# Layer 2 attention scores of a four-layer model: weighted spectra made four products ahead, one sample pair's softmax between the other pair's products

## The chip, the cores and the metric

The kernel runs on one core of a Trainium2 chip, in one launch. The metric is the device time of that launch in microseconds (us). A core has TensorE (PE, matrix products, with its weight loads listed as PEld), VectorE (DVE), ScalarE (ACT), GpSimd (POOL), and SyncE (SP), which here only issues transfers. All data are 32-bit floats. Engines run their own instruction lists in order and wait for each other through semaphores.

## The reference

The input is x of shape (4, 56, 56, 128). Four layers follow one another, each as `x = x + layer(groupnorm(x))`: window and full attention with an MLP, an edge layer, a spectral attention (layer 2), and a small convolution. The change is in layer 2. It sees each of the 4 samples as 56 images t of 56 x 128 and does, with 32 heads:

```python
k = _fno_layer(xa_n, wK, ...)     # spectral convolution to half size, 32 heads
q = _fno_layer(xa_n, wQ, ...)
v = _fno_layer(xa_n, wV, ...)     # full size
scores = einsum('bhtd,bhsd->bhts', qs, ks) / sqrt(d)
attn_w = softmax(scores, axis=-1)
out = einsum('bhts,bhsd->bhtd', attn_w, vs)
projd = _fno_layer(out, wP, ...)  # back to one image
attention = _inorm(projd + xa, ...)
```

followed by two more spectral layers. An `_fno_layer` multiplies an image's low frequencies with weights of the head, transforms back, and adds a weighted copy of the image (the skip).

## The kernel before

The kernel never makes q and k. By Parseval's theorem a score is a sum over frequencies: the image spectra of t times those of s, weighted per head and frequency with a product of the two weight sets. `spectra` (a function before the change) leaves in on-chip memory, for two sample pairs `bp` and two samples `b2` in the two halves of 64 partitions, `st.S` (spectra in 16 columns c, 56 times t), `st.iS` (the same times i), `st.R` (17 columns of the other frequencies, which only the skips need), and in device memory `st.apart` (four rows that need an own product). `all_score_weights` leaves the weights `st.g`, `st.g4`.

`attention_weights` (L1383 and on) then works for each sample pair:

- skips (L1411 to L1421): 17 columns, for each sample two matmuls of 64 x 64 tiles into `q_pg`; ScalarE copies (L1420) and GpSimd multiplies with `ww`, per head (L1421), into `q_sc`.
- weighted spectra `q_u` (128 partitions x 32 heads x 56): for each column c a real one (n=0) and an imaginary one (n=1). The real ones are made by VectorE (L1448), which reads the spectrum from a copy `q_px` in the matmul banks (PSUM); GpSimd makes the imaginary ones from `st.iS` for c below 12 (L1445), VectorE the last four. Each tag of `q_u` has three buffers.
- products (`add`, L1435): each `q_u` is multiplied with `st.S` by 8 matmuls, over two row halves (the two samples) and two column halves of PE's array, into `q_acc`, four banks. After the 32 of S come four with `T` and `Tp`, from VectorE (L1454), over all 128 rows.
- softmax (L1458 to L1467): VectorE adds `q_acc` to `q_sc`, reduces, subtracts, ScalarE takes the exponential, VectorE reduces, inverts and multiplies.

After both pairs, all scores are transposed into `st.AT` (L1477, copies by VectorE and ScalarE in turn), `eye` is made by GpSimd, and 32 matmuls with it give `AbT`, the mixing matrix (L1490). Order in this stage comes from a scheduler that places instructions by priority, save where `manual_schedule` holds engines to program order.

`attend` follows: 24 turns of weighting the value spectra `xh` with `u_d`, rows of a table `dd` that SP loads and spreads over partitions (L1517), by VectorE (L1544, from a copy `u_px` that ScalarE makes, L1528) and GpSimd (L1546), and of matmuls with `st.AT` (L1549). PE and ScalarE are held to program order here. In the middle of each turn it runs a step of `mix_images`, which mixes the input images with `AbT` and writes them out: 18 steps.

On-chip memory is a stack from the left and one from the right. A tile that takes freed memory waits for the last use of what lay there. `q_T`, `q_Tp`, `q_sc` and the `q_u` lie left, over the memory of the spectra stage; `u_d` takes it after them.

Of the kernel before, what the change touches and what calls it, by code (L numbers as in the profile page):

```python
# [18 lines left out]
P = 128  # L19
# [1364 lines left out]
def attention_weights(k, I, w, st):  # L1384
# [4 lines left out]

    nc, tc = k.nc, k.tc  # L1390
    g, g4 = st.g, st.g4
    with ExitStack() as es:
        big = es.enter_context(tc.tile_pool(name="q_big", bufs=1))
        wks = ExitStack()
        wk = wks.enter_context(tc.tile_pool(name="q_wk", bufs=2))
# [8 lines left out]
        nc.vector.tensor_mul(ww, w.qksh[:, 0, :], w.qksh[:, 1, :])  # L1404
        pv = big.tile([112, 16], F32, name="q_pv")
        nc.vector.tensor_mul(pv, w.pva[:, 0, :], w.pva[:, 1, :])
        halves = (slice(0, 64), slice(64, 128))
        sc = big.tile([P, B, 16, HH], F32, name="q_sc")

        with tc.tile_pool(name="q_ps0", bufs=2, space=PSUM) as psum:  # L1410
            for bp in range(2):  # L1411
                pg = [psum.tile([P, 512], F32, name="q_pg%d" % b2) for b2 in range(2)]
                for c in range(17):
                    for b2 in range(2):
                        r = st.R[halves[b2], bp, c, :]
                        for o in halves:
                            nc.tensor.matmul(pg[b2][o, :HH], r, r[:, :HH], start=(c == 0), stop=(c == 16))
                for b2 in range(2):
                    g0 = wk.tile([P, HH], F32, name="q_g0")
                    nc.scalar.copy(g0, pg[b2][:, :HH])  # L1420
                    nc.gpsimd.tensor_mul(sc[:, 2 * bp + b2], bc(g0, 1, 16), bc(ww, 2, HH))  # L1421
        with tc.tile_pool(name="q_ps", bufs=1, space=PSUM) as psum:
            for bp in range(2):
                px = psum.tile([P, 3, 512], F32, name="q_px")
                for i in range(2):
                    nc.scalar.copy(px[:, i, :NB].rearrange("p (c t) -> p c t", t=HH), st.S[:, bp, 8 * i:8 * i + 8, :HH])
                nc.scalar.copy(px[:, 2, :4 * HH].rearrange("p (c t) -> p c t", t=HH), st.iS[:, bp, 12:16, :HH])
                acc = psum.tile([P, 4, 512], F32, name="q_acc")

                def add(u, x, rows, b2, start=False, stop=False):  # L1430
                    for hb in range(4):
                        for i in range(2):
                            if b2 is None or b2 == i:
                                o = halves[i] if rows is None else rows
                                nc.tensor.matmul(acc[halves[hb % 2], 2 * i + hb // 2, :NB], x[o],  # L1435
                                                 u[o, 8 * hb:8 * hb + 8, :].rearrange("p h t -> p (h t)"),
                                                 start=start, stop=stop)


                for c in range(16):  # L1440
                    for n in range(2):
                        u = wk.tile([P, HEADS, HH], F32, tag="u%d" % (n and c < 12), name="q_u", bufs=3)
                        weights = bc(g[:, n, c, :], 2, HH)
                        if n and c < 12:
                            nc.gpsimd.tensor_mul(u, bc(st.iS[:, bp, c, :HH], 1, HEADS), weights)  # L1445
                        else:
                            x = px[:, 2, (c - 12) * HH:] if n else px[:, c // 8, c % 8 * HH:]
                            nc.vector.tensor_mul(u, bc(x[:, :HH], 1, HEADS), weights)  # L1448
                        add(u, st.S[:, bp, c, :], None, None, start=(c == 0 and n == 0))
                for b2 in range(2):  # L1450
                    b = 2 * bp + b2
                    for n in range(2):
                        u = wk.tile([P, HEADS, HH], F32, tag="u0", name="q_u4", bufs=3)
                        nc.vector.tensor_mul(u, bc(Tp[:, n, b, :HH], 1, HEADS), bc(g4[:, n, 0, :], 2, HH))  # L1454
                        add(u, T[:, b, :], slice(0, P), b2, stop=(n == 1))
                scp = sc[:, 2 * bp:2 * bp + 2]
                scf = scp.rearrange("p b (x h) s -> p (b x) (h s)", x=2)
                nc.vector.tensor_add(scf, scf, acc[:, :, :NB])  # L1458
                scf = scp.rearrange("p b i s -> p (b i) s")
                red = wk.tile([P, 2 * 16], F32, tag="red", name="q_red")  # L1460
                nc.vector.tensor_reduce(red, scf, AX.X, ALU.max)
                nc.vector.tensor_sub(scf, scf, bc(red, 2, HH))
                nc.scalar.activation(scf, scf, AF.Exp, scale=1.0 / math.sqrt(ND))
                den = wk.tile([P, 2 * 16], F32, tag="red", name="q_den")
                nc.vector.tensor_reduce(den, scf, AX.X, ALU.add)
                nc.vector.reciprocal(den, den)
                nc.vector.tensor_mul(scf, scf, bc(den, 2, HH))  # L1467
        wks.close()
        big = es.enter_context(tc.tile_pool(name="q_end", bufs=1))
        with tc.tile_pool(name="q_ps1", bufs=2, space=PSUM) as psum:  # L1470
            at = st.AT.rearrange("p (i f) b t -> p b i f t", f=2)
            for b in range(B):
                for i0 in range(0, 8, 4):
                    pt = psum.tile([P, 4, P], F32, name="q_pt")
                    for i in range(4):
                        ii = 2 * (i0 + i)
                        nc.tensor.transpose(pt[:112, i, :], sc[:, b, ii:ii + 2, :].rearrange("p h s -> p (h s)"), k.ident)  # L1477
                    for i in range(4):
                        copy(k, i, at[:, b, i0 + i], pt[:112, i, :].rearrange("p (f t) -> p f t", f=2)[:, :, :at.shape[4]])
            eye = big.tile([112, 16, HH], F32, name="q_eye")  # L1480
            fold = big.tile([112, HH], F32, name="q_fold")
            nc.sync.dma_start(fold[:HH], I["w2_eye"])
            nc.sync.dma_start(fold[HH:], I["w2_eye"])
            nc.gpsimd.tensor_mul(eye, bc(fold, 1, 16), bc(pv, 2, HH))
            pa = psum.tile([P, 2, 64], F32, name="q_pa")
            nc.vector.memset(st.AbT, 0.0)
            for b2 in range(2):
                o = slice(64 * b2, 64 * b2 + HH)
                for hp in range(16):
                    nc.tensor.matmul(pa[o], eye[:, hp, :], st.AT[:, hp, b2::2, :], start=(hp == 0), stop=(hp == 15))  # L1490
                nc.scalar.copy(st.AbT[o], pa[o, :, :HH])


def attend(k, st, dd, xad, xm):

    nc, tc = k.nc, k.tc
# [928 lines left out]
```

## Time and profile before

| | |
|---|---|
| median of 3 runs | 3965.18 us (3956.41 to 3967.73) |
| profiled execution | 3959.12 us, span 3957.3 us |
| granted PE clock, mean | 0.952 |
| busy: PE, DVE, ACT, POOL | 3558.4, 2896.4, 2048.5, 1181.2 us |
| end of the spectra's matmuls, first product `q_acc` | 3037.9, 3054.89 us |
| last division of the softmax begins | 3189.81 us |
| first `u_po` matmul of the value stage | 3219.93 us |

Times inside the span count from its start. A page of the profile gives busy time by engine, the span in 40 slices, the chain of work that ended last, and groups of instructions; the trace can be asked for stretches, single tiles, waits and the timeline. A timeline row reads: start in us, length in us, engine, line, operation, out<-in, shapes, count, and in brackets the idle time before it and what ended that. A tile row gives durations as smallest/median/largest in ns, and first and last start. Matmul lengths are modelled at their end; their starts are measured. Each matmul has two records.

### The profile page before, as it was taken

How to read it: one execution, taken by the hardware profiler on the slowest of the kernel's cores; microseconds unless marked ns; L12 is line 12 of the kernel's file. 1: busy time of each engine (PE TensorE's matmuls, PEld its weight loads, DVE VectorE, ACT ScalarE, POOL GpSimd, SP SyncE). 2: the span in 40 equal slices, each digit the busy share in tenths (PEclk: the TensorE clock that was granted, in tenths of full speed). 3: DMA queues.
4: the chain of work that ended last, by engine and by line, in shares of the span. 5: the costliest groups of instructions: out<-in, count | busy, mean ns of one | idle time of the engine just before them, and what ended most of it. 6: DMA issues, size and time to landing. Idle time of an engine off the chain costs nothing. (4 is left out here: it accounts for less than half of the span.)

```text
span 3957.3 us, 79405 instructions
## 1 busy us (share of the span) xinstructions
PE 3558.4 (90%) x35416; PEld 1586.4 (40%) x35416; DVE 2896.4 (73%) x2678; ACT 2048.5 (52%) x2067; POOL 1181.2 (30%) x664
## 2 busy tenths in 40 slices
PE   6899988989998898999889899998967969999988
PEld 4322234542223445222245532224545333336554
DVE  6588868758887685898778578886874857775664
ACT  4577754557775455777545477764522012215332
POOL 0000007500000670000057000003742648984665
PEclk8999989999999999999999999999977989999988
DMA  2000000000000000000000000000031047832101
GB/s 94 1 1 1 1 1 19 19 1 1 1 1 1 18 19 1 1 1 1 1 18 3 17 1 1 1 1 1 3 132 39 1 94 166 173 90 82 58 9 49
DMA packets 73496, 111.12 MB, mean 28 GB/s; under 512 B 62140, under 2 KB 63932, under 8 KB 67900
## 3 DMA queue, kind: packets, MB, share of 16 engines
q1 hardware_dynamic: 14460, 93.13, 7.9%
q10 hardware_dynamic: 58688, 12.85, 1.9%
q8 instruction: 279, 4.57, 0.5%
q14 instruction: 69, 0.57, 0.0%
HBM read 79.46 MB, written 26.51 MB: 27 GB/s over the span
## 5 line engine op out<-in xcount | busy, mean ns | idle before, releaser
L641 ACT ACTIVATE f_ring<-f_s 128x1792 f32<-128x1792 f32 (+3 forms) x796 | 1097.9, 1429 | 316.9 <-PE f_s L639 314.8
L594 DVE TENSOR_TENSOR f_acc<-f_acc,f_ring 128x1792 f32<-128x1792 f32 x560 | 1134.0, 2025 | 81.1 <-ACT f_ring L641 27.7
L639 PE MATMUL f_s<-f_qT,f_kT 32*128 32x448 f32 x5376 | 740.6, 573 | 57.7 <-ACT f_ring L641 26.6
L883 POOL TENSOR_TENSOR x<-xf,xw 128x343 f32<-128x343 f32 (+2 forms) x36 | 29.9, 832 | 2131.7 <-issue 2059.4
L600 PE MATMUL f_po<-f_ring,f_va 128*32 128x448 f32 x5376 | 592.1, 548 | 0.0
L967 DVE TENSOR_TENSOR e_td<-e_pa,e_c 128x1792 f32<-128x1792 f32 x252 | 491.2, 2012 | 8.0 <-ACT e_a L934 8.0
L969 POOL TENSOR_TENSOR e_tp<-e_a,e_c 128x1792 f32<-128x1792 f32 x140 | 451.7, 3258 | 143.4 <-PE e_acc L974 104.6
L639 PEld LDWEIGHTS f_s<-f_qT,f_kT 32*128 32x128 f32 x5376 | 268.6, 184 | 538.7 <-ACT f_ring L641 369.6
L974 PE MATMUL e_acc<-e_td,t_shared 32*32 32x448 f32 x8064 | 322.3, 545 | 25.3 <-DVE e_td L967 14.8
L971 ACT ACTIVATE e_tp<-e_tp 128x1792 f32<-128x1792 f32 x140 | 235.1, 1697 | 186.6 <-POOL e_tp L969 186.6
L1544 DVE TENSOR_TENSOR u_ud<-u_px,u_d 112x1792 f32<-112x1792 f32 x144 | 240.2, 1707 | 106.3 <-PE u_po L1549 82.7
L600 PEld LDWEIGHTS f_po<-f_ring,f_va 128*32 128x32 f32 x5376 | 133.0, 109 | 399.8 <-issue 398.9
L1549 PE MATMUL u_po<-u_ud,AT 112*64 112x448 f32 x960 | 202.2, 551 | 34.5 <-DVE u_ud L1544 34.5
L974 PE MATMUL e_acc<-e_tp,t_shared 32*32 32x448 f32 x4480 | 220.6, 544 | 2.4 <-ACT e_tp L971 2.2
L1546 POOL TENSOR_TENSOR u_up<-xh,u_d 112x1792 f32<-112x1792 f32 x64 | 193.4, 3046 | 48.2 <-PE u_po L1549 21.2
L974 PEld LDWEIGHTS e_acc<-e_td,t_shared 32*32 32x32 f32 x8064 | 133.6, 103 | 149.8 <-DVE e_td L967 59.9
L594 DVE TENSOR_TENSOR f_acc<-f_ring 128x1792 f32<-128x1792 f32 x28 | 56.7, 2024 | 106.3 <-ACT f_ring L641 77.4
L1549 PEld LDWEIGHTS u_po<-u_ud,AT 112*64 112x64 f32 x960 | 65.2, 138 | 159.6 <-issue 87.5
L1549 PE MATMUL u_po<-u_up,AT 112*64 112x448 f32 x576 | 126.2, 545 | 0.0
L1435 PE MATMUL q_acc<-q_u,S 64*64 64x448 f32 x1024 | 102.6, 557 | 16.6 <-DVE q_u L1448 12.5
L974 PEld LDWEIGHTS e_acc<-e_tp,t_shared 32*32 32x32 f32 x4480 | 94.4, 103 | 54.7 <-ACT e_tp L971 18.5
L1445 POOL TENSOR_TENSOR q_u<-iS,q_g 128x1792 f32<-128x1792 f32 x24 | 77.6, 3268 | 124.5 <-PE s_px L1282 92.8
(462 smaller groups left out, 4721.7 us busy)
## 6 DMA issues: line engine op xcount, KB each, us to landing
u_d<-dd SPq DMA_DIRECT2D x48, 784.0 KB
xw<-in_x SPq DMA_DIRECT2D x4, 1568.0 KB
x2d<-x SPq DMA_DIRECT2D x4, 1568.0 KB
x_xs<-xad ACTq DMA_DIRECT2D x32, 196.0 KB
xm<-x_ev ACTq DMA_DIRECT2D x64, 98.0 KB
o_a<-xm SPq DMA_DIRECT2D x8, 784.0 KB
o_x<-x2d SPq DMA_DIRECT2D x4, 1568.0 KB
out<-o_o SPq DMA_DIRECT2D x12, 448.0 KB
```

What stands on the lines that cost most here:

```text
L594: nc.vector.tensor_add(acc, slots(j, 0) if c == 1 else acc, slots(j, c))
L600: nc.tensor.matmul(po[heads[h], :NB], va[o, c, heads[h]], p, start=(c == 0), stop=(c == 24))
L639: nc.tensor.matmul(ss[:, i, :NB], kT[heads[h], c * P:(c + 1) * P], qT[heads[h], blk(j)], start=True, stop=True)
L641: nc.scalar.activation(ring[:, slot:slot + m, :], ss[:, :m, :NB], AF.Exp, scale=scale)
L967: nc.vector.tensor_tensor(t, am, cm, ALU.max)
L969: nc.gpsimd.tensor_sub(t, bc(a.rearrange("p (l n) -> p l n", l=8), 1, 4), cm)
L971: nc.scalar.activation(tf, tf, AF.Relu)
L974: nc.tensor.matmul(acc[quarters[q], r, :NB], k.ident[o, o], t[o, q].rearrange("p l n -> p (l n)"), start=(g == 0), stop=(g == len(EDGE_TUR ...
L1435: nc.tensor.matmul(acc[halves[hb % 2], 2 * i + hb // 2, :NB], x[o], u[o, 8 * hb:8 * hb + 8, :].rearrange("p h t -> p (h t)"), start=start, ...
L1544: nc.vector.tensor_mul(u, bc(px[:, :, :NB], 2, m), dm)
L1546: nc.gpsimd.tensor_mul(u, bc(x, 2, m), dm)
L1549: nc.tensor.matmul(po[64 * b2:64 * b2 + 64, :NB], st.AT[:, 8 * i + h0 + q, 2 * bp + b2, :], u[:, b2, q, :], start=(left == 16), stop=(left ...
```

## The change

- One list `seq` holds 36 products for each pair; a `T` product stands before the imaginary one of every fourth column.
- `make` is called for the product four places further on before each product. Copies `q_px` are made for eight columns at a time, in two buffers. All imaginary `q_u` are made by GpSimd.
- `product` loops over the sample outside and the four head blocks inside. Each sample has its own `q_acc` of two banks, one buffer.
- `skips`, `softmax` and the transposes are generators that advance one step after each product from the fourth on: the skips of both pairs between the products of the first pair, the softmax and transposes of the first pair between those of the second. VectorE multiplies the skips with `ww`, straight from `q_pg`; the softmax works on one sample at a time; ScalarE alone copies transposes, four at once.
- Four engines are held to program order in the whole stage.
- `q_T`, `q_Tp`, `q_ww` and `q_sc` lie right.
- `pv`, `fold`, `eye` and the `AbT` matmuls go to `mix_images`, in its first and a new second step (19 steps now); the matmuls alternate between the column halves. The memset of `AbT` is GpSimd's.

```diff
-        big = es.enter_context(tc.tile_pool(name="q_big", bufs=1))
-        wks = ExitStack()
-        wk = wks.enter_context(tc.tile_pool(name="q_wk", bufs=2))
+        big = es.enter_context(tc.tile_pool(name="q_big", bufs=1, side="right"))
+        wk = es.enter_context(tc.tile_pool(name="q_wk", bufs=2))
+        psum = es.enter_context(tc.tile_pool(name="q_ps", bufs=2, space=PSUM))
...
+        es.enter_context(tc.manual_schedule(engines={mybir.EngineType.PE, mybir.EngineType.Activation,
+                                                      mybir.EngineType.DVE, mybir.EngineType.Pool}))
+        px, made, acc = {}, {}, {}
+        seq = []
+        for bp in range(2):
+            for c in range(16):
+                seq += [(bp, c, 0, None), (bp, c, 1, None)]
+                if c % 4 == 3:
+                    seq.insert(len(seq) - 1, (bp, None, c // 4 % 2, c // 8))
+
+        def make(bp, c, n, b2):
+            if b2 is None and n == 0 and c % 8 == 0:
+                px[bp, c // 8] = t = psum.tile([P, 512], F32, tag="x", name="q_px")
+                nc.scalar.copy(t[:, :NB].rearrange("p (c t) -> p c t", t=HH), st.S[:, bp, c:c + 8, :HH])
+            u = wk.tile([P, HEADS, HH], F32, tag="u%d" % (b2 is None and n), name="q_u", bufs=3)
+            if b2 is not None:
+                nc.vector.tensor_mul(u, bc(Tp[:, n, 2 * bp + b2, :HH], 1, HEADS), bc(g4[:, n, 0, :], 2, HH))
+            elif n:
+                nc.gpsimd.tensor_mul(u, bc(st.iS[:, bp, c, :HH], 1, HEADS), bc(g[:, n, c, :], 2, HH))
+            else:
+                nc.vector.tensor_mul(u, bc(px[bp, c // 8][:, c % 8 * HH:c % 8 * HH + HH], 1, HEADS),
+                                     bc(g[:, n, c, :], 2, HH))
...
+        def product(bp, c, n, b2):
...
+                acc[bp] = [psum.tile([P, 2, 512], F32, tag="acc%d" % i, name="q_acc", bufs=1) for i in range(2)]
+            for i in range(2):
+                if b2 is None or b2 == i:
+                    x, o = (st.S[:, bp, c, :], halves[i]) if b2 is None else (T[:, 2 * bp + b2, :], slice(0, P))
+                    for hb in range(4):
+                        nc.tensor.matmul(acc[bp][i][halves[hb % 2], hb // 2, :NB], x[o],
+                                         u[o, 8 * hb:8 * hb + 8, :].rearrange("p h t -> p (h t)"),
+                                         start=first, stop=last)
...
+        def softmax(bp, copies):
+            red, den = {}, {}
+            for i in range(2):
+                red[i] = wk.tile([P, 16], F32, tag="red", name="q_red")
+                nc.vector.tensor_reduce(red[i], sc[:, 2 * bp + i], AX.X, ALU.max)
+                nc.vector.tensor_sub(sc[:, 2 * bp + i], sc[:, 2 * bp + i], bc(red[i], 2, HH))
+                nc.scalar.activation(sc[:, 2 * bp + i], sc[:, 2 * bp + i], AF.Exp, scale=1.0 / math.sqrt(ND))
+                yield
+            for i in range(2):
+                den[i] = wk.tile([P, 16], F32, tag="den", name="q_den")
+                nc.vector.tensor_reduce(den[i], sc[:, 2 * bp + i], AX.X, ALU.add)
+                nc.vector.reciprocal(den[i], den[i])
+                nc.vector.tensor_mul(sc[:, 2 * bp + i], sc[:, 2 * bp + i], bc(den[i], 2, HH))
+                yield
...
+                    for q in range(4):
...
+                    copies(at[:, b, i0:i0 + 4], pt[:112].rearrange("p i (f t) -> p i f t", f=2))
+                    yield
+
+        between = [skips(0), skips(1)]
+        ahead = 4
+        for item in seq[:ahead]:
+            make(*item)
+        for n, item in enumerate(seq):
+            if n + ahead < len(seq):
+                make(*seq[n + ahead])
+            product(*item)
+            if item[1:3] == (15, 1):
+                for i in range(2):
+                    collect(item[0], i)
+                between.append(softmax(item[0], nc.scalar.copy))
+            if n >= 3 and between and next(between[0], 0) == 0:
+                between.pop(0)
...
 def mix_images(k, I, w, st, wk, psum, xad, xm):
...
+    eye = wk.tile([P, 2, 8, HH], F32, tag="x_ev", name="x_eye", bufs=1)[:112].rearrange("p b w h -> p (b w) h")
+    nc.gpsimd.tensor_mul(eye, bc(fold, 1, 16), bc(pv, 2, HH))
     load(0)
     load(1)
+    yield
+    pa = bank()
+    for hp in range(16):
+        for b2, o in enumerate(halves):
+            nc.tensor.matmul(pa[o, 0, :2 * 64].rearrange("p (b t) -> p b t", b=2), eye[:, hp, :], st.AT[:, hp, b2::2, :],
+                             start=(hp == 0), stop=(hp == 15))
+    for o in halves:
+        nc.scalar.copy(st.AbT[o], pa[o, 0, :2 * 64].rearrange("p (b t) -> p b t", b=2)[:, :, :HH])
```

## The prediction

> **What bounds the kernel now.** I first read the table of stretches, to find the stage that the change touches and which engine fills it. Columns: length of the stretch, busy time and records of each engine, granted TensorE clock, DMA share.
>
> ```profile
> core 0: us, PE busy (x) PEld busy (x) DVE busy (x) ACT busy (x) POOL busy (x), PEclk, DMA share, GB/s
> 3038.00:3055.00 17.00, 4.52 (x276) 4.29 (x280) 2.45 (x4) 2.68 (x8) 16.07 (x7) 0.80 0.09 25
> 3055.00:3108.00 53.00, 52.32 (x520) 18.95 (x520) 41.43 (x22) 2.71 (x4) 37.86 (x12) 0.97 0.01 1
> 3108.00:3118.00 10.00, 5.38 (x28) 1.66 (x32) 10.00 (x7) 0.00 (x0) 0.00 (x0) 0.92 0.00 1
> 3118.00:3130.00 12.00, 12.00 (x104) 4.31 (x104) 11.90 (x7) 1.70 (x1) 6.14 (x2) 0.78 0.00 1
> 3130.00:3181.00 51.00, 46.59 (x448) 16.99 (x440) 43.20 (x23) 0.00 (x0) 24.06 (x8) 1.00 0.00 1
> 3181.00:3198.00 17.00, 7.33 (x33) 5.17 (x34) 12.26 (x22) 5.59 (x17) 5.75 (x3) 0.61 0.01 3
> 3198.00:3208.00 10.00, 9.11 (x64) 8.61 (x64) 0.00 (x0) 0.74 (x3) 0.00 (x0) 0.82 0.00 0
> 3208.00:3225.00 17.00, 5.07 (x14) 1.71 (x16) 5.05 (x3) 1.50 (x2) 6.01 (x2) 0.62 0.88 203
> ```
>
> The score stage lies from 3038.6 (last matmul of the spectra) to about 3208. PE is full in the two product stretches. Around them lie 17 us in which GpSimd works (skips) and PE does 4.5 us; 10 us of one sample pair's end; 34 us of softmax, transposes and `AbT`, one after the other; and 12 us of waiting for `u_d`. What ends that last wait is in the chain of waits in order of time (start, length, what):
>
> ```profile
> 3197.85 5.57 PE q_pa L1490 x32
> ...
> 3203.74 3.71 PE q_pa L1490 x32
> ...
> 3207.94 9.52 DMA u_d<-dd
> ...
> 3217.85 2.04 DVE u_ud L1544
> ...
> 3219.93 9.02 PE u_po L1549 x32
> ```
>
> The value stage's first matmul is at 3219.93. It stood behind a load issued at 3207.58 (12.35 us earlier), and the load behind the `AbT` matmuls, whose memory it takes. Then the timeline and the tiles, for durations:
>
> ```profile
> 3064.39 2.02 DVE L1448 TENSOR_TENSOR q_u<-q_px,q_g 128x1792 f32<-128x1792 f32 x1 [0.98 <-PE q_acc L1435]
> ...
> 3094.46 9.75 DVE L1448 TENSOR_TENSOR q_u<-q_px,q_g 128x1792 f32<-128x1792 f32 x5 [0.98 <-PE q_acc L1435]
> ...
> 3117.79 0.30 PEld L1435 LDWEIGHTS q_acc<-q_u,S 64*64 64x64 f32 x8 [4.84 <-DVE q_sc L1458]
> ...
> 3123.86 11.28 POOL L1445 TENSOR_TENSOR q_u<-iS,q_g 128x1792 f32<-128x1792 f32 x3 [26.00 <-PE q_acc L1435]
> ...
> 3127.94 4.15 DVE L1467 TENSOR_TENSOR q_sc<-q_sc,q_den 128x1792 f32<-128x1792 f32 x1
> ```
>
> ```profile
> L1448 DVE TENSOR_TENSOR q_u<-q_px,q_g x40: 2006/2020/2026, 3052.8 to 3167.7; 128x1792 f32<-128x1792 f32 x40
> L1445 POOL TENSOR_TENSOR q_u<-iS,q_g x24: 3187/3195/4975, 3038.2 to 3150.9; 128x1792 f32<-128x1792 f32 x24
> L1467 DVE TENSOR_TENSOR q_sc<-q_sc,q_den x2: 2008/3079/4150, 3127.9 to 3189.8; 128x1792 f32<-128x1792 f32 x2
> ```
>
> From 3064.39 to 3094.46 VectorE is released ten times by PE, each time after two products: 30.07/20 = **1.504 us for a product** at full clock. A weighted spectrum costs 2.02 on VectorE (1.94 start to start in the run of five), 3.16 start to start on GpSimd.
>
> **Part 1: the front.** The first product waits today for skips and all three `px` copies (3054.89). New: one `px` copy (0.54 us, L1426) after ScalarE's last `xh` copy at 3038.55, then 2.02 on VectorE: 3041.2; I take 3041.3. The skips' matmuls come after four products: 136 records a pair, at 223 records in 3.48 us = 2.1 us; I use 2.0 (the row holds a pause). Their products with `ww` go from GpSimd (4 x 1.69) to VectorE, half a big operation (1.0 each), behind PE. `ww`, `pv` and the memset are under 0.2 us, cost nothing, and lie before the products. The loads of `T` and `Tp` (nine on SP, done issuing by 3043.4 today) are first needed at the eighth product, about 3052: hidden.
>
> **Part 2: a sample pair.** 16 re, 16 im and 4 of `T`: 36 x 1.504 = 54.1 us of PE. The four `T` products now stand amid the others and change the tile shape twice each. The nearest row is the first layer's attention: matmuls 0.376 apart, but 0.48 at the change of shape (last L639 start 2301.32, first L600 start 2301.80), so 0.11 a change, 0.9 a pair. Bounds: 0 and 0.2. First pair: 54.1 + 0.9 + 2 skips (4.0) = 59.1, ending **3100.4**. VectorE has there 20 x 1.94 + 4.0 = 43, GpSimd 16 x 3.16 = 51: both hidden by PE, with three buffers each.
>
> All im products on GpSimd (32 instead of 24) and `T` products, subtraction and division on VectorE meanwhile: the division row says what this costs. At 3127.94 it took 4.15 us instead of 2.01, as GpSimd's running operation ended at 3130.2, and GpSimd's next took 4.98. Before, no `T` product or subtraction met GpSimd: it was idle. By the row alone only divisions are charged. The Trainium skill, "SBUF — State Buffer", Who interferes with whom, states that any VectorE instruction with two SBUF inputs locks out a reading GpSimd one, wholly: then the 8 `T` products and 4 subtractions join. By the rule GpSimd needs 32 x 3.16 + 8 x 2.0 + 4 x 1.0 = 121 us, done at 3159, still ahead of PE; by the row 103. I take the rule: a wait before each such VectorE operation of 0 to 3.16, 1.6 taken.
>
> **Part 3: the seam.** One accumulator, so PE waits for both `collect`s (2 x 1.0 + 0.3): 3102.7, against 4.1 today. Softmax of pair 0 then stands between products, in order. VectorE: two collects 2.0, reduce 1.0, subtract 1.0, a product 1.94, reduce, subtract, reduce (3.0), reciprocal 0.25, divide 1.0 = 10.2, plus three waits for GpSimd 4.8 = 15.0, so the first division ends at 3115.6. On PE, four products (6.0) after 3102.7 end at 3108.7; there the first **transpose waits, and all later products behind it, 7.0 us** (2.3 if no wait for GpSimd, 11.7 at the worst waits). Today's stall of 4.07 us before 3117.79 let the clock fall: 0.78 over the next 12 us, 2.6 us lost. I add 2.6 (0 to 3.4). Exps (half of 1.70) run beside VectorE; the table load precedes them.
>
> Second pair: 54.1 + 0.9 + four transpose groups. Each has 8 records of 128 columns, 0.109 apart at full clock (second half of L1490), 0.87, and two shape changes: 1.1. So 59.4. End of products: 3102.7 + 59.4 + 7.0 + 2.6 = **3171.7**.
>
> **Part 4: the tail.** Softmax of pair 1 is bare: eight VectorE half operations (8.2), two reciprocals 0.5, two collects 2.0, hops 0.4: last division ends 3182.8 (from 3179.25 to 3191.82, 12.6 us, today).
>
> The moved step: in the changed program the first `u_d` load waits, on SP, for exactly this division, whose divisor's memory it takes; no longer for transposes and `AbT`. Ahead of it on SP are the two `x_fold` loads (kilobytes), which wait for the last product, earlier. So issue 3182.8, then the same 12.35 to the first `u_po` matmul: **3195.2**. The last transposes and ScalarE's copies (about 5 us), `u_px` behind them on ScalarE (0.9), `eye` and two `u_x` on GpSimd (1.7 + 4.1) lie under the load's 10.3 us; without it, some 6 us would show. The `x_xs` loads on ScalarE's queue come after `u_px`, as before.
>
> Saved: 3219.93 − 3195.2 = 24.7.
>
> **Part 5: given back.** `AbT` moves into the second turn of the value stage, where PE waits only 22 us for VectorE in 335. 64 records alternate two column halves: 64 x 0.109/2 = 3.5 us, plus the wait for two ScalarE copies before `pn` may take the same bank, 0.7: **4.2** (7.7 if the halves don't overlap, 0 if absorbed). Mixing uses 19 of 24 turns instead of 18: nothing.
>
> **Sum.** −24.7 + 4.2 = −20.5. Profiled execution: 3959.12 (span 3957.3) to 3938.6. The median of the runs, 3965.18, lies 6.1 above that execution; I carry the difference over: **3944.7**.
>
> **A rule against the change.** `product` now gives a row half its four matmuls in succession (tiles A B A B C D C D; before A C B D A C B D). The row first: 16 records of a product in four groups of four starts, 0.376 apart, though every matmul has two records. The Trainium skill, "TensorE: Matmul & The Clock Gate", Part 3, says matmuls start and end strictly in program order. Record by record this would make a product 8 groups = 3.0 us in both orders; the row shows 1.504, so the rule doesn't hold for records here. Holding for whole matmuls it lets C start with the second A, D with the second B, and the next A with the second C: again four to a group. I take 1.504.
>
> **Rivals.**
> - *The new order costs PE its overlap* (the other side): if C waits for the second A to finish, a product has 6 groups, 2.26 us; 64 of them cost 48 us more, so 3993. It decides from 20.5/64 = 0.32 us a product, 1.83 us, on. For it: no row shows one tile twice before another row half. Against: the skips, two matmuls per row half in succession, ran four to 62 ns (223 in 3.48 us).
> - *The seam is cheap*: no clock fall, no shape cost, short waits for GpSimd: 2.6 + 2.7 + 4.7 + 1 = 11 less: 3934. For it: ScalarE and PE have little else there. GpSimd's 3159 is the floor.
> - *The seam and waits are dear*: worst waits (+4.7), shape changes at 0.2 (+2), `AbT` not overlapped (+3.5): 3955. For it: GpSimd is almost never idle, so waits are the rule.
>
> **How the numbers follow.** Mine 0.63 (3937 to 3952), cheap seam 0.15, dear 0.15, order 0.07. A measurement tells 0.3% (12 us) from no change, so "faster" ends at 3953.3. Faster: 0.61 + 0.15 + 0.05 = 0.81; same: 0.02 + 0.10 = 0.12; slower 0.07. Range: from inside the cheap case, 3929, to past the dear one, 3960.
>
> **What would show it.** First `q_acc` matmul near 3041; products 1.5 us apart; VectorE's `T` products of 2 to 5 us and GpSimd's between 3.2 and 5.2; one PE gap of 5 to 10 us before the first `q_pt`; `u_d` issued right after the last division; first `u_po` near 3195. Wrong if products are over 1.8 us apart, GpSimd ends after PE, or the value stage, 340 us from first `u_po` to 3560, grows by over 6 us.

## The result, and the profile after

The changed kernel takes **3935.36 us** (median of 4 runs, 3929.22 to 3944.01) against 3960.8 for the kernel before, measured beside it: a ratio of 0.9937, 95% interval 0.9909 to 0.9964. Its profiled execution took 3933.23 us with a span of 3931.4, 25.9 less than the 3957.3 before. I had forecast 3944.7 for the median and 20.5 us less for the span.

First the table of stretches of the changed kernel, cut where its stage has its own seams (same columns as in the prediction):

```profile
core 0: us, PE busy (x) PEld busy (x) DVE busy (x) ACT busy (x) POOL busy (x), PEclk, DMA share, GB/s
3036.00:3039.30 3.30, 0.02 (x2) 0.02 (x2) 2.10 (x2) 1.53 (x3) 3.10 (x2) 1.00 0.29 80
3039.30:3101.00 61.70, 61.52 (x816) 29.91 (x816) 55.30 (x26) 0.54 (x1) 59.47 (x18) 0.97 0.01 4
3101.00:3170.00 69.00, 61.08 (x560) 27.91 (x560) 57.86 (x32) 5.96 (x8) 50.63 (x16) 0.95 0.01 1
3170.00:3193.00 23.00, 3.91 (x18) 3.14 (x18) 12.45 (x14) 5.99 (x8) 8.08 (x4) 0.55 0.47 105
```

The 17 us without a product at the front are 3.3 now. Pair 0 (second row) keeps PE full, and VectorE and GpSimd nearly so. Pair 1 has 8 us of PE idle in 69. After it lie 23 us with 4 us of PE, where before 28.9 us (last product to load) and then 12.4 us of load stood; the prediction's 34 us for the first of these was too much. The end of the stage, in the chain of waits in order of time (start, length, what):

```profile
3179.42 1.10 DVE q_sc L1480
3180.89 9.75 DMA u_d<-dd
3190.86 2.04 DVE u_ud L1561
3192.94 6.41 PE u_po L1566 x24
...
3214.81 3.52 PE x_po L1616 x64
3218.91 0.58 PE x_po L1627 x8
3220.29 6.36 PE u_po L1566 x24
```

The load follows the last division at once, with no transpose or `AbT` between. `AbT`'s matmuls (L1616) now stand in the value stage's second turn. Last the tiles, where the durations changed (smallest/median/largest in ns):

```profile
L1432 POOL TENSOR_TENSOR q_u<-iS,q_g x32: 3183/3192/4982, 3036.4 to 3159.1; 128x1792 f32<-128x1792 f32 x32
L1434 DVE TENSOR_TENSOR q_u<-q_px,q_g x32: 2006/2014/2025, 3037.2 to 3156.3; 128x1792 f32<-128x1792 f32 x32
L1430 DVE TENSOR_TENSOR q_u<-q_Tp,q_g x8: 2018/4324/5037, 3045.9 to 3159.3; 128x1792 f32<-128x1792 f32 x8
L1473 DVE TENSOR_TENSOR q_sc<-q_sc,q_red x4: 1091/1460/2695, 3104.0 to 3174.6; 128x896 f32<-128x896 f32 x4
L1480 DVE TENSOR_TENSOR q_sc<-q_sc,q_den x4: 1091/1092/2678, 3112.0 to 3179.4; 128x896 f32<-128x896 f32 x4
```

A real `q_u` (one operand in PSUM) never takes more than 2.03 us on VectorE; a `T` product of the same size (both operands in on-chip memory) takes 4.3 in the median and up to 5.04.

The timeline of the seam, which answers to the stall at 3117.79 before:

```profile
3103.96 2.69 DVE L1473 TENSOR_TENSOR q_sc<-q_sc,q_red 128x896 f32<-128x896 f32 x1
3112.02 2.68 DVE L1480 TENSOR_TENSOR q_sc<-q_sc,q_den 128x896 f32<-128x896 f32 x1
3114.76 1.10 PE L1488 MATMUL q_pt<-t_shared,q_sc 128*112 128x128 f32 x4 [5.54 <-DVE q_sc L1480]
```

PE waits 5.54 us for the first transpose, and two operations of the chain that it waits for take 1.6 us more than they need.

Where the 25.9 us went, from the record starts of both traces:

| step | before | after | difference |
|---|---|---|---|
| start of the span to the end of the last `xh` copy | 3038.53 | 3036.55 | −1.98 |
| to the first product | 16.36 | 2.74 | −13.62 |
| first to last `q_acc` matmul | 123.77 | 128.78 | +5.01 |
| to the end of the last division | 13.16 | 12.44 | −0.72 |
| to the issue of the first `u_d` load | 15.76 | 0.03 | −15.73 |
| to the first `u_po` matmul | 12.35 | 12.41 | +0.06 |
| first to last `u_po` matmul | 341.16 | 342.08 | +0.92 |
| to the end | 396.17 | 396.34 | +0.17 |

The first row is code that the change doesn't touch: in the experiments below it ranges from 3031.5 to 3044.1, and the last row from 393 to 415. So the experiments are compared by the **stage**, from the end of the last `xh` copy to the first `u_po` matmul: 181.40 us before, 156.40 after. Its parts repeat to a few hundredths from run to run where the clock is the same. What a run adds to the value stage is told beside it.

### The profile page after: what moved, and what is told of

It reads as the page before. It is cut to its first block, busy times and chain, and to the rows that moved or that the text cites. A ratio compares the mean times of both kernels' runs of the same rounds, so it can differ in the third digit from the quotient of the medians.

```text
span 3931.4 us, 79382 instructions
## 1 busy us (share of the span) xinstructions
PE 3547.4 (90%) x35416; PEld 1589.8 (40%) x35416; DVE 2900.7 (74%) x2667; ACT 2048.0 (52%) x2055; POOL 1211.2 (31%) x671
## 5 line engine op out<-in xcount | busy, mean ns | idle before, releaser
L1432 POOL TENSOR_TENSOR q_u<-iS,q_g 128x1792 f32<-128x1792 f32 x32 | 112.8, 3557 | 13.1 <-PE q_acc L1447 13.1
L856 ACT ACTIVATE m_hT<-m_ph,w_fb 128x392 f32<-128x392 f32 x128 | 72.7, 589 | 73.6 <-PE m_ph L855 68.1
```

## The experiments

**The order of a product's matmuls** (rival "the new order costs PE its overlap"). A harder order than the change's own: the two matmuls of one tile next to each other.

```diff
-                    for hb in range(4):
+                    for hb in (0, 2, 1, 3):
                         nc.tensor.matmul(acc[bp][i][halves[hb % 2], hb // 2, :NB], x[o],
```

> Stage length is counted from the end of the last xh copy to the first u_po matmul: 156.4 us in the changed kernel (3036.55 to 3192.94). Here the two matmuls of one tile of PE's array stand next to each other (A A B B C C D D). Theory 1, which the prediction used: matmuls start in order, a matmul waits only for the one before it on its own tile, each holds a tile for 0.752 us. Then a product takes four such slots, 3.0 us instead of 1.504: 64 x 1.5 = +96 us, the eight T products +0.75 each, less the 5.5 us of the seam that a slower PE no longer shows: stage +90 to +100, about 4030 us in all. Theory 2, PE takes any matmul whose tile is free, in whatever order they come: a product stays at 1.5 us and the time at 3933.

Measured: stage 158.32, time 3947.45 with a first row of 3040.8 and a last of 404.1. Theory 2 holds. The time from one product to the next, taken from the starts of the matmul records (products 8 to 16 of pair 0, us; the 16th is a `T` product):

```
order A B A B C D C D:  1.51 1.50 1.50 1.50 1.50 1.50 1.50 1.66
order A A B B C C D D:  1.51 1.50 1.50 1.50 1.50 1.50 1.50 1.76
```

In the second order, too, the records come in groups of four, the groups 0.376 apart. The four of a group start within 0.17 us (most groups), in the changed kernel within 0.07, in the kernel before within 0.02: the order leaves a mark, but costs these products nothing. Were matmuls started in the listed order, D could not begin with A. The records don't name their tiles; their times fit a PE that passes over matmuls that wait for their tile. Only the step to a `T` product, which has two tiles instead of four, takes 0.1 us more, eight times. Most of the rest of the 1.9 us lies at the seam, where the clock came back later (products 40 to 42). So the order was never a danger here, and my argument for it ("holding for whole matmuls") was wrong too: neither records nor matmuls hold it.

**The front undone.** Both pairs' skips first, copied by ScalarE and multiplied by GpSimd, as before.

```diff
-        between = [skips(0), skips(1)]
+        for bp in range(2):
+            for _ in skips(bp):
+                pass
+        between = []
...
-                nc.vector.tensor_mul(sc[:, 2 * bp + i], bc(pg[i][:, :HH], 1, 16), bc(ww, 2, HH))
+                t = wk.tile([P, HH], F32, tag="sk", name="q_sk", bufs=2)
+                nc.scalar.copy(t, pg[i][:, :HH])
+                nc.gpsimd.tensor_mul(sc[:, 2 * bp + i], bc(t, 1, 16), bc(ww, 2, HH))
```

> All skips stand ahead of the first product again, copied by ScalarE and multiplied by GpSimd, as before the change; the rest is the changed kernel. Theory 1: PE has the same work, the loss is that GpSimd's four operations (4 x 1.69) come before its first q_u, so that it runs behind PE through pair 0 and ends it near 3104 instead of 3100.8: stage 156.4 + 3 to 5 = 160. Theory 2: the 13.6 us by which the first product came earlier are a gain of their own, and go with the skips: stage 170.

Measured: stage 161.95, +5.55; pair 0's last product starts 4.7 us later (67.21 after the copy, not 62.53). A little over theory 1's 3 to 5, far from theory 2. Theory 1's reason, a GpSimd that runs behind PE through the pair, holds only in part. PE waits at the first two products, and at no later one of pair 0:

```profile
3045.26 2.68 PE L1447 MATMUL q_acc<-q_u,S 64*64 64x448 f32 x16 [3.01 <-DVE q_u L1434]
3049.16 11.07 PE L1447 MATMUL q_acc<-q_u,S 64*64 64x448 f32 x96 [1.21 <-POOL q_u L1432]
```

The 3.01 us are for VectorE's first `q_u`, whose `q_px` copy stands on ScalarE behind the copies of the skips. Only the 1.21 are GpSimd's late start. The first product starts 6.16 us later than in the changed kernel, and 4.0 of these come back because the skips only moved. So of the 4.7 us 2.2 are the later first product, 1.2 the wait for GpSimd, and the other 1.3 fit the clock: without the wait the first three products take 2.69, 3.04 and 1.79 us, in the changed kernel 3.04, 1.70 and 1.50.

The kernel before, with the same skips ahead, had its first product at 16.36, not at 8.90. There GpSimd made three `q_u` before it came to the skips, and ScalarE's last copies, with `q_px` behind them, waited for it:

```profile
3038.18 9.49 POOL L1445 TENSOR_TENSOR q_u<-iS,q_g 128x1792 f32<-128x1792 f32 x3 [92.77 <-PE s_px L1282]
3047.64 6.62 POOL L1421 TENSOR_TENSOR q_sc<-q_g,q_ww 128x896 f32<-128x896 f32 x4
3049.36 0.20 ACT L1420 COPY q_g<-q_pg 128x56 f32<-128x56 f32 x1 [8.06 <-POOL q_sc L1421]
```

So of the 13.6 us by which the first product came earlier, 7.5 lie in that order, 4.0 are skips that only moved, and 2.2 are the rest of what the skips held up. On the whole stage this edit, the skips' place and their engines together, is worth 5.5 us; no run parts the two.

**`AbT` back ahead of the load.** `eye` (in a `q_u` buffer) and the 64 matmul records at the end of the score stage, so that `u_d` takes their memory as before.

```diff
+        eye = wk.tile([P, HEADS, HH], F32, tag="u0", name="q_eye", bufs=3)[:112, :16]
+        nc.gpsimd.tensor_mul(eye, bc(fold, 1, 16), bc(pv, 2, HH))
         for steps in between:
...
+        pa = psum.tile([P, 2, 128], F32, tag="x", name="x_po")
+        for hp in range(16):
...
-    yield
-    pa = bank()
```

> eye and AbT's matmuls stand at the end of the score stage again, as before the change, and eye lies in memory that u_d takes. Theory 1: the load waits for the last transposes' copies (3183.2 in the changed kernel) and 5.5 us of AbT, so first u_po comes 8 us later, stage 164.5; the value stage loses AbT's 4.1 us in its second turn but has its mixing step in the first again: 341. Sum +7. Theory 2: the load's start is no bound (other work of the value stage's start takes as long): stage 158 or less, sum below +1.

Measured: stage 168.24, value stage 342.33. From the last division to the load it takes 6.84 us instead of 0.03, and the load itself 12.70: theory 1, 7 of the expected 8. But the stage grew by 11.8. Most of the other 4.7 us come from an accident that shows something else. A `T` product is made on VectorE while GpSimd runs six `q_u` in a row (3.19 each for the first five, without a gap):

```profile
3047.71 8.47 DVE L1435 TENSOR_TENSOR q_u<-q_Tp,q_g 128x1792 f32<-128x1792 f32 x1 [0.75 <-issue]
3038.50 20.73 POOL L1437 TENSOR_TENSOR q_u<-iS,q_g 128x1792 f32<-128x1792 f32 x6
```

It began 0.3 us before the end of one of these and waited for the two after it as well: 6.45 us beyond its 2.02. PE stood still for 0.63 and 2.04 us of it and came out 4.5 us behind the changed kernel; the rest of that fits the clock (the skip matmuls after the second wait took 2.76 us instead of 2.15, the next product 2.62 instead of 1.51).

The value stage, which no longer holds `AbT`, was expected at 341 and took 342.33. The next experiment shows why.

**`AbT` in the first turn of the value stage instead of the second.**

```diff
     load(1)
-    yield
     pa = bank()
```

> AbT's 64 matmul records run in the first turn of the value stage instead of the second. The value stage (first to last u_po matmul) took 341.2 us before the change and 342.1 after it, although AbT's 4 us of PE came into it. Theory 1: what the second turn saved is a wait; in the first turn VectorE stands at the mixing's copies x_n with no product made ahead, in the second it has two ready. Then this kernel's value stage is 3 us longer, 345. Theory 2: AbT's matmuls cost the same in any turn, and the missing 3 us came from the clock: 342.

Measured: value stage 341.90, first turn 21.87 us and second 13.77 (changed kernel: 15.63 and 20.17; before: 21.15 and 13.77). The turn doesn't matter: theory 1 is out, and theory 2's number is right. Its reason is only half right. In the kernel before, VectorE was held by the mixing's copies `x_n` with a value product queued behind them, and PE waited for that product; here `AbT`'s matmuls stand in that place, and the products are made meanwhile. The first three rows are the kernel before, the last fence is this run:

```profile
3229.69 0.57 PE L1595 MATMUL x_po<-c_ones,norm 1*56 1x1 f32 x8 [0.25 <-DVE x_n L1597]
3230.49 2.02 DVE L1544 TENSOR_TENSOR u_ud<-u_px,u_d 112x1792 f32<-112x1792 f32 x1
3232.57 3.25 PE L1549 MATMUL u_po<-u_ud,AT 112*64 112x448 f32 x8 [2.31 <-DVE u_ud L1544]
```

```profile
3202.72 3.96 DVE L1561 TENSOR_TENSOR u_ud<-u_px,u_d 112x1792 f32<-112x1792 f32 x2 [2.06 <-PE u_po L1566]
3204.01 3.66 PE L1615 MATMUL x_po<-AT,x_eye 112*56 112x128 f32 x64
3209.58 2.96 PE L1566 MATMUL u_po<-u_ud,AT 112*64 112x448 f32 x8
```

3.66 us of matmuls and 0.60 of waiting for the `AbT` copies came in, 2.31 of waiting went out: +1.95. The rest fits the clock. At full clock a group of eight `u_po` records starts 1.50 or 1.55 us after the one before it, at a granted clock of 0.50 it is 3.04. What the groups of the first two turns took beyond 1.50 or 1.55 (those with other work between them left out) sums to:

| kernel | beyond full clock, us | 1.95 and the clock make | measured against before |
|---|---|---|---|
| before | 4.4 | | |
| changed | 3.6 | +1.1 | +0.9 |
| changed, again (below) | 3.2 | +0.8 | +0.6 |
| this run | 3.4 | +0.9 | +0.7 |
| `AbT` ahead of the load (no 1.95) | 5.6 | +1.2 | +1.2 |

The kernel before pays twice, behind the load and behind its 2.31 us of waiting (3.04 for the next group). Of the two runs of the changed kernel one pays at the start and after `AbT`, the other at the start alone, so a part of this is chance. No run holds the clock still.

**Pair 0's softmax spread over pair 1.** One step at every fifth product, and the transposes from the 21st on.

```diff
-            if n >= 3 and between and next(between[0], 0) == 0:
+            due = n < 35 or n > 56 or n % 5 == 0
+            if n >= 3 and between and due and next(between[0], 0) == 0:
```

> Pair 0's softmax advances at every fifth product of pair 1 instead of at each of the first four, and its transposes follow from the 21st product on. Theory 1: the changed kernel's 5.5 us of PE waiting for the first transpose and the half clock after it (1.6 us) come only from VectorE's 14 us of softmax being asked for within six us of products; spread, none of it shows: last q_acc matmul 6 to 7 us sooner after the last xh copy (131.5 to about 125). Theory 2: VectorE and GpSimd are too full in pair 1 to take the softmax anywhere (they block each other): products wait instead, and at most 2 us are gained. A clock lower or higher at the stage's start (1.5 us between runs so far) is to be taken off first.

Measured: last `q_acc` matmul at 131.03, that is 0.5 sooner. Theory 2. The wait before the first transpose is gone, and others stand in its place:

```profile
3105.24 4.30 DVE L1430 TENSOR_TENSOR q_u<-q_Tp,q_g 128x1792 f32<-128x1792 f32 x1
3109.59 1.72 PE L1447 MATMUL q_acc<-q_u,q_T 128*64 128x448 f32 x8 [1.07 <-DVE q_u L1430]
3110.57 2.97 DVE L1473 TENSOR_TENSOR q_sc<-q_sc,q_red 128x896 f32<-128x896 f32 x1
3115.53 12.50 PE L1447 MATMUL q_acc<-q_u,S 64*64 64x448 f32 x112 [2.54 <-DVE q_u L1434]
```

A `T` product of 4.30 and a subtraction of 2.97, 2.3 and 1.9 more than they take alone, are what PE waits for. Is that VectorE's work, or its waits for GpSimd? The run with PSUM operands below answers it.

**The load early.** The softmax's small tiles lie in the right-hand memory.

```diff
-                red[i] = wk.tile([P, 16], F32, tag="red", name="q_red")
+                red[i] = big.tile([P, 16], F32, tag="red", name="q_red", bufs=2)
...
-                den[i] = wk.tile([P, 16], F32, tag="den", name="q_den")
+                den[i] = big.tile([P, 16], F32, tag="den", name="q_den", bufs=2)
```

> q_red and q_den lie in the right-hand memory, so that the first u_d load takes nothing of the softmax and waits for the last product instead of the last division. Theory 1: the load starts 12 us sooner and is done before the last transposes' copies (147 us after the last xh copy); then these, u_px (0.9) and one q_ud product (2.0) bound: first u_po at 149.7 instead of 156.4, 6.7 us gained. Theory 2: the load's start isn't the bound, GpSimd's u_x or the copies are: under 2 us gained.

Measured: stage 148.76, 7.6 us shorter, as theory 1 has it; the load is issued at 132.05 instead of 143.99. The value stage gives 2.5 back (344.57): 4.2 in its first turn (19.85 instead of 15.63), less 1.7 in the second (18.50 instead of 20.17):

```profile
3181.21 4.12 POOL L1542 TENSOR_TENSOR u_x<-xh 112x896 f32<-112x896 f32 x2 [12.85 <-PE q_pt L1488]
3185.27 6.02 POOL L1563 TENSOR_TENSOR u_up<-xh,u_d 112x1792 f32<-112x1792 f32 x2
3189.31 3.25 PE L1566 MATMUL u_po<-u_up,AT 112*64 112x448 f32 x8 [1.31 <-POOL u_up L1563]
```

GpSimd still makes two `u_x` (needed four turns later) once the last transposes free their memory. They had lain under the load; now `u_up` and PE wait 1.31 behind them, and PE stays at half clock for two groups more (3.25 where 1.84 stood). What the early load uncovers is what I had listed as lying under it. In the run with all edits below, the wait is there again (1.30), the clock is full behind it, and the value stage takes 341.53: of the 2.5 us only the wait repeats.

**Pair 0's skip matmuls ahead of the first product.**

```diff
         between = [skips(0), skips(1)]
+        next(between[0])
```

> The skip matmuls of pair 0 stand ahead of the first product, their multiplications stay where they are. Theory 1: PE is idle for the 2.7 us until the first q_u is there, so 2.0 us of skips fit in, and PE's clock has no gap to fall in: last q_acc matmul 2.0 us sooner, 3.5 with the clock. Theory 2: the skips' banks come free only with the last xh copy and run at half clock, so that they push the first product to about 4 us: at most 0.7 gained.

Measured: the first product still starts at 2.73, pair 0's last product at 58.81 instead of 62.53: 3.7 sooner, theory 1 with the clock (product 1 comes 1.55 after product 0, in the changed kernel 3.04). At the end of pair 1, however, only 1.4 is left (130.14), where 2.0 to 3.5 was expected. The seam took back 1.5 us at the first subtraction, which met GpSimd's operation at a worse moment:

```profile
3103.90 4.15 DVE L1473 TENSOR_TENSOR q_sc<-q_sc,q_red 128x896 f32<-128x896 f32 x1
```

4.15 against 2.69 in the changed kernel, where it takes 1.09 alone; what remains is the clock after the longer wait.

**PSUM operands.** The small broadcast operand of each VectorE operation that meets GpSimd goes to PSUM: `g4` beside the spectra in `q_px`, `q_red` and `q_den` in a bank of their own. (They leave `u_d`'s memory too, hence the comparison with the early load.)

```diff
+                nc.scalar.copy(t[:, NB:NB + 2 * HEADS].rearrange("p (n h) -> p n h", n=2), g4[:, :, 0, :])
...
-                nc.vector.tensor_mul(u, bc(Tp[:, n, 2 * bp + b2, :HH], 1, HEADS), bc(g4[:, n, 0, :], 2, HH))
+                nc.vector.tensor_mul(u, bc(Tp[:, n, 2 * bp + b2, :HH], 1, HEADS),
+                                     bc(px[bp, b2][:, NB + HEADS * n:NB + HEADS * n + HEADS], 2, HH))
...
+            rd = psum.tile([P, 512], F32, tag="t", name="q_rd")
...
-                red[i] = wk.tile([P, 16], F32, tag="red", name="q_red")
+                red[i] = rd[:, 16 * i:16 * i + 16]
...
-                den[i] = wk.tile([P, 16], F32, tag="den", name="q_den")
+                den[i] = rd[:, 32 + 16 * i:48 + 16 * i]
```

> The changed kernel with the weights g4 of the T products, q_red and q_den in the matmul banks (PSUM), so that no VectorE operation beside GpSimd's has two operands in on-chip memory; q_red and q_den leave the memory that u_d takes, so its load starts early, and the run is to be compared with e3_load_early. Theory 1: VectorE's waits for GpSimd's running operation come from the two operands: all eight T products take 2.0 us (2.0 to 5.0 in the changed kernel), the four subtractions and divisions 1.1 (two of 2.7), GpSimd's q_u 3.2 (up to 5.0), and the 5.5 us wait before the first transpose becomes 2.3, the last q_acc matmul coming 3 to 4 us sooner than the 131.3 of e3. Theory 2: any VectorE operation that writes or reads on-chip memory beside GpSimd can be held up, and the spread of durations stays: 131.

The tiles of this run, and its first transpose:

```profile
L1434 POOL TENSOR_TENSOR q_u<-iS,q_g x32: 3191/3194/3201, 3040.9 to 3160.9; 128x1792 f32<-128x1792 f32 x32
L1431 DVE TENSOR_TENSOR q_u<-q_Tp,q_px x8: 2011/2020/2022, 3050.4 to 3162.1; 128x1792 f32<-128x1792 f32 x8
L1476 DVE TENSOR_TENSOR q_sc<-q_sc,q_rd x4: 1086/1086/1087, 3108.4 to 3176.8; 128x896 f32<-128x896 f32 x4
L1483 DVE TENSOR_TENSOR q_sc<-q_sc,q_rd x4: 1086/1086/1087, 3115.1 to 3182.0; 128x896 f32<-128x896 f32 x4
```

```profile
3116.27 1.10 PE L1491 MATMUL q_pt<-t_shared,q_sc 128*112 128x128 f32 x4 [2.57 <-DVE q_sc L1483]
```

Theory 1: not one of the 48 operations deviates by more than 0.02 us, on either engine, and the wait is 2.57 where the changed kernel shows 5.54. The last `q_acc` matmul comes at 129.81, only 1.5 sooner than in the early-load run, not 3 to 4: 3.0 of wait are gone, but the first product starts 0.25 later (a copy more ahead of it), and after the shorter wait the clock stays low for one product longer (4.24 instead of 3.21 us from product 40 to 41). The stage is 147.89, 0.9 shorter than with the early load alone, the value stage 343.12. The operands in PSUM are not quite free: from the last `q_acc` matmul to the end of the last division it takes 12.25 us instead of 11.71, as VectorE's steps there start 0.1 to 0.2 us further apart.

**All of it together**, first without the PSUM operands, then with them.

> The three edits together: softmax of pair 0 spread, load early, skips of pair 0 first. If they are independent (theory 1) the stage from the last xh copy to the first u_po is 156.4 - 7 - 6.7 - 2 = 141, and the time about 3918 against 3933. Theory 2, they share a bound (a load that is early meets the end of the spectra's chain, a VectorE that is busier elsewhere): less than two thirds of that, stage 146 or more.

> e9_all (softmax spread, load early, skips of pair 0 first) with the PSUM operands of e7. Theory 1: what kept the spread softmax from paying (products that waited at the 43rd, 45th and 52nd place) were VectorE's waits for GpSimd; without them pair 1's products run at 1.5 us and the last q_acc matmul comes at 121 to 124 after the last xh copy (128.2 in e9, 131.5 in the changed kernel), first u_po at 139 to 142. Theory 2: VectorE's work itself (16 q_u, 4 T products and 14 us of softmax in 60 us) is the bound: 127 or more.

Without: last `q_acc` matmul at 128.20, first `u_po` at 145.65, so 10.7 of the 15.7 us that the parts were to give: just short of theory 2's 146, and far from theory 1's 141. Products still wait at places 43, 45 and 52 (3.09, 4.28 and 3.00 us). With the PSUM operands they come 2.22, 1.55 and 1.66 apart, the last `q_acc` matmul at 121.20 and the first `u_po` at 139.29. The worth of the spread softmax can be read from pair 1 alone, from its first product to its last matmul. While VectorE waits for GpSimd it is small: 66.09 us in the changed kernel and 65.77 spread, or 68.41 and 66.48 with pair 0's skips first. With the PSUM operands it is 5.1: 64.40 and 59.26.

**Timed, beside the changed kernel**, on one chip in five rounds.

> The changed kernel once more, on the chip of the next run. The time was 0.9937 of the kernel before. Expected the same again, 0.9937 within 0.003; the stage from the last xh copy to the first u_po 155 to 157 us, and whatever else differs from run to run lies in stages that the change doesn't touch.

> The kernel of e10_best, timed. From the last xh copy to the last u_po matmul it took 480.8 us against 498.5 of the changed kernel and 522.6 of the kernel before. If the stages around keep their time (theory 1), it is 41.8 us faster than before, 0.9895, and 17.7 faster than the changed kernel. Theory 2: a PE that waits less is given less clock later on, and half of the second gain is lost: 0.9915.

| kernel | median, us | ratio to the kernel before (95%) | stage | value stage |
|---|---|---|---|---|
| before | 3960.58 (11 runs) | | 181.40 | 341.16 |
| changed, again | 3934.95 (6 runs) | 0.9939 (0.9925 to 0.9954) | 156.51 | 341.74 |
| all edits with PSUM operands | 3921.21 (5 runs) | 0.9904 (0.9889 to 0.9919) | 139.29 | 341.74 |

The changed kernel repeats. The last kernel beats both; its interval holds both theories' ratios (0.9895 and 0.9915), so the times don't tell whether some of the gain is given back. Its profile doesn't show it: value stage and rest (396.38) are those of the changed kernel to 0.02 us.

## Why the prediction was right

The direction, the mechanisms and the order of size were right; the span fell by 25.9 where 20.5 was forecast. Of the 5.4 us, 2.0 are the drift ahead of the stage, 3.3 the value stage. The median lay 9.3 under the forecast; 4.4 of that is the kernel before, whose median a fourth run brought from 3965.18 to 3960.8. The stage itself was forecast at 156.65 from the end of the last `xh` copy (3195.2 − 3038.55) and measured at 156.40. So close a hit is luck, since errors of up to 3.5 us cancelled:

- **Front (part 1).** 2.75 to the first product, measured 2.74. But "16 re, 16 im and 4 of `T`: 36 x 1.504" took the full clock from the first matmul on. PE had been idle for 3.3 us, and the first product took 3.04, at a granted clock of 0.50: 1.5 us that I had left out. I had charged the clock after the seam only. My reading of the front before was wrong too: of GpSimd's 16.07 us only 6.62 were skips, 9.49 were three `q_u`.
- **Change of tile shape (part 2).** From one `T` product to the next it is 13.89 us for nine products, 0.36 above 9 x 1.504, four times a pair; I had 0.22, with 0.4 as the bound.
- **GpSimd (part 2).** The choice between row and rule fell right: beside GpSimd not only a division can be held, but any VectorE operation with two operands in on-chip memory (here seven of eight `T` products and three of the eight subtractions and divisions), as the section Who interferes with whom of the Trainium skill's page "SBUF — State Buffer" has it; the run with PSUM operands shows that it is the operands. GpSimd's 32 `q_u` took 113.8 us in sum (mean 3557 ns), 11.6 more than with the PSUM operands (102.2); the row alone would add 2, the rule 20. My bound "a wait of 0 to 3.16" was too narrow: 6.45 was measured where GpSimd's operations follow one another without a gap.
- **Seam (part 3).** "One accumulator, so PE waits for both `collect`s" is wrong: each sample has its own, and PE went on after the first, 1.16 us instead of 2.3. That gained nothing, since the second sample's matmuls ran about 1.1 us behind and the first transpose waits for VectorE in any case. The first transpose waited 5.54 instead of 7.0, since two of three operations met GpSimd (1.6 each), not all three. After it PE lost about 1.4 to the clock (0.45 in the transposes, 0.96 in the product) instead of 2.6. A group of transposes costs 0.75, not 1.1: its four transposes have one record each, not two, as the rows of the kernel before show as well (32 for 32).
- **Tail (part 4).** From the last product's end (3168.61) to the last division 11.9, forecast 11.1; the difference is a subtraction of 1.83 that met GpSimd's `x_eye` (1.09 where `eye` was made earlier, with `AbT` ahead of the load). The load and its 12.35 us came as said (12.4).
- **Given back (part 5).** This step failed in size: 4.2 forecast, 0.9 measured (0.6 in the second run). I priced the matmuls that came in and not the wait that stood in their place before: PE's 2.31 us for a value product behind `x_n`, with the low clock behind it.
- **Rivals.** The order rival is out by a far harder order. The cheap seam was not it either: stalls and clock were there. From the end of pair 0 to the end of the products it took 67.8 us instead of 71.3, and pair 0 itself 61.5 instead of 59.1.

The forecast didn't ask which part pays. The seam doesn't: PE's waits and low clock there (1.2, 5.5 and 1.4) come to 8.1 us, without the 1.1 in which one sample's matmuls ran alone, against 6.7 before (4.07 and 2.6). Skips behind products, on their new engines, are worth 5.5 us of the stage, the rest of the new order at the front 7.5 us to the first product, and `AbT` behind the load 6.8 from division to load. The rest of the 15.7 us between division and load, about 9, I put down to the transposes and copies that left the tail; no run took them alone. If that is so, pair 0's softmax between the products pays only there, until VectorE no longer waits for GpSimd.

## What to carry to other kernels

Before VectorE and GpSimd are to work side by side, list VectorE's operations with both inputs in on-chip memory: each can cost one or two whole GpSimd operations, and a small broadcast operand put in PSUM took that cost away here, for 0.1 to 0.2 us a step where the steps hang on each other. When work moves into a stage, price what stood still in its place, not only what comes in; and when a tile's memory is handed on, look at which small tile keeps the next load waiting: here 64 bytes a partition held back a load by 12 us.

## What the runs showed of the hardware

- PE does not hold matmuls of different tiles to their listed order: with the two of one tile next to each other, records still start in groups of four, 0.376 us from group to group and 0.17 within one, and a product takes 1.50 us; in the listed order it would take 4 x 0.752 = 3.0.
- A VectorE operation that is held by GpSimd can lose to two of its operations in succession: 8.47 us for 2.02 of work.
- 3.3 us without a matmul were enough for a first product at half speed (3.04 us instead of 1.50, at a granted clock of 0.50) in seven of eight runs, and with the front undone 3.0 us were enough for two slow ones (2.69 and 3.04). With 2.2 us of skip matmuls in the gap none of four runs showed it.
